# Moving two ScalarE-issued stores, of B and of the time step, later in the recorded program of a Mamba layer

## The chip, the cores and the metric

The kernel runs on one core of a Trainium2 chip. The metric is the device time of one execution in microseconds (us), and the kernel before and after the change are compared by medians of such times. All data are float32.

## The reference

Four layers are applied one after the other to an image `x` of shape (2, 128, 64, 64). The change lies in the last one, layer 3, a small selective-state-space model (Mamba) that runs over the channels of each pixel. The 128 channels of a pixel are a sequence of 8 tokens with 16 features. Cut to what matters:

```python
seq = x.transpose(0, 2, 3, 1).reshape(B * H * W, 8, 16)
xi, z = split(seq @ in_proj_w.T)                  # 32 inner features each
xs  = silu(causal_conv4(xi))
dt, Bm, Cm = split(xs @ x_proj_w.T, [1, 17])      # 1 + 16 + 16 columns
dt  = softplus(dt @ dt_proj_w.T + dt_proj_b)      # the time step
dA  = exp(dt[..., None] * A)                      # A = -exp(A_log), 16 states
dBx = dt[..., None] * Bm[:, :, None, :] * xs[..., None]
h_t = dA_t * h_{t-1} + dBx_t                      # 8 tokens, one after the other
y_t = sum over states of h_t * C_t
out = ((y + xs * D) * silu(z)) @ out_proj_w.T
result = x + silu(group_norm(out) * gn_gamma + gn_beta)
```

The layers before it are a Mamba over the image (layer 0) and two attention layers (1 and 2). The diff does not touch them.

## The kernel before

Layer 3 handles the 8192 pixels in 16 chunks of T = 512 pixels (`Chunk3`, called chunk 0 to chunk 15 here). A chunk holds two halves `i` of four tokens each, with 4 tokens x 32 inner features on the 128 partitions.

The scan over the 8 tokens is cut into 4 steps of two tokens (`PLACE`), so the main loop has 16 x 4 steps plus a few at the ends, counted by `s`. In a step the token pair needs the state-times-feature layout: 128 partitions hold 4 states x 32 features, and 4 groups of them cover the 16 states. Getting from one layout to the other means copying rows to many partitions, and this is done through device memory (DRAM):

- `b_` computes B on TensorE (into the PSUM tile `misc`) and copies it to `bs` on ScalarE, and ScalarE's queue stores it as the DRAM tile `rows` (256 KB, line L1193).
- `dt_add` adds the time step on GpSimd (L1217), and `put` stores it from ScalarE's queue as the DRAM tile `ddt` (512 KB, L1224).
- `spread(k)` (L1232) loads the time step of a token pair from `ddt` into `dtr`, in 8 DMAs of 64 KB (4 in step 0). `load(k, o)` (L1244) loads B of one token from `rows` into `D`, in 4 DMAs of 256 KB. Both are issued by SyncE (SP in the profile), two steps ahead of the step that uses them (`n2`).
- `da_` (L1273) makes the four exponentials `A` from `dtr` on ScalarE, one step ahead. `db_` (L1266) multiplies `D` with the time step times input on VectorE, also one step ahead.
- `mul` (L1283, GpSimd) and `add` (L1288, VectorE and GpSimd) carry the state over the tokens, and `hc_` (L1306, VectorE) and `y_` (L1316, TensorE) multiply by C and sum.
- In the first eight steps a 512 KB store of the input for later use, `kept` (L1483), is also issued by SyncE.

The order of the work is written by hand. The loop puts work in lists keyed by (step in chunk, quarter of the step): `first` runs at the start of a quarter, `extra` at its end, and `PLAN` orders the vector work in between. B and the time step of the next chunk (`fut`) are made in step 0 of the current one: `b_` in quarter 0, `put` in quarter 2. The lines are

```python
more((0, 0), fut.b_, at=first)
more((0, 1), fut.c_, at=first)
more((0, 2), fut.put, fut.cb_)
...
more((k, 0), lambda: n2.spread(n2k), lambda: n2.load(n2k, 0))
more((k, 1), lambda: n2.load(n2k, 1))
```

Two more things of the built program matter. First, each engine runs its own instructions in order. Second, the layer below the kernel's text (Tile) gives the DMAs of both issuing queues completion semaphores from one ring of eight, in the order in which it places the DMAs in the program. Before a DMA takes a semaphore, its issuing engine waits until the DMA that had the semaphore before, eight places earlier, has landed (a wait that the engine has already made is left out). So a DMA on SyncE can wait for a store that ScalarE issues, though it touches none of the same data.

Of the kernel before, what the change touches and what calls it, by code (L numbers as in the profile page):

```python
# [57 lines left out]
def conv_seq_kernel(ctx: ExitStack, tc: tile.TileContext, a: dict, out: bass.AP):  # L58
# [40 lines left out]
    with ExitStack() as c0:  # L99
# [9 lines left out]
        def wt(tag, bufs=None, shape=(P, 2, T)):  # L109
            return wk_.tile(list(shape), F32, tag=tag, name=tag, bufs=bufs)  # L110
# [386 lines left out]
        with tc.manual_schedule():  # L497
            c, c1 = chunks[:2]
# [234 lines left out]
    with ExitStack() as c1:  # L733
# [272 lines left out]
        for n, j in enumerate(jobs):  # L1006
# [10 lines left out]
            if jobs[n - 1].layer == 1:  # L1017
                for ci in range(NCH):
                    c = Conv(jobs[n - 1].b, ci)
# [70 lines left out]
    with ExitStack() as c3:  # L1090
# [61 lines left out]
        class Chunk3:  # L1152
# [35 lines left out]
            def b_(self):  # L1188
                p = self.bc_(0)
                self.bs = wt("bs", (P, T), bufs=1)  # L1190
                nc.scalar.copy(self.bs, p)
                self.rows = dr.tile([P, T], F32, tag="rows", name="rows")
                nc.scalar.dma_start(self.rows, self.bs)  # L1193

            def c_(self):
# [222 lines left out]
        with tc.manual_schedule():  # L1418
            mm(y, lhsT=ident, rhs=x[:, 0, 0:T], start=True, stop=True)
            c, c1 = chunks[:2]  # L1420
            for i in range(2):
                c.xs_(i)
            c.b_()
            for i in range(2):
                c.dt_(i)
            c.e_exp()
# [15 lines left out]
            for s in range(-1, len(steps) + 3):  # L1442
# [3 lines left out]
                fut = chunks[ci + 1] if s >= 0 and ci + 1 < len(chunks) else None  # L1446
# [8 lines left out]
                def more(key, *what, at=extra):  # L1455
                    at.setdefault(key, []).extend(what)

                if fut is not None:
                    more((0, 0), fut.b_, at=first)
                    more((0, 1), fut.c_, at=first)  # L1460
                    more((0, 2), fut.put, fut.cb_)
                if old is not None:
                    more((1, 0), lambda: old.yg_(1))
                    more((2, 1), old.xr_, at=first)
# [199 lines left out]
```

## Time and profile before

| what | value |
|---|---|
| median of 3 runs | 6684.76 us (6681.85 to 6688.01) |
| the profiled execution | 6684.23 us, of which the span on the core is 6682.4 us |
| busy over the span | PE 88%, DVE 83%, ACT 67%, POOL 81% |
| layer 3's loop, from the first `rows` store | from 5645 us to the end of the span |
| busy from 5640 to 6630 us (990 us) | PE 811.8, DVE 820.9, POOL 772.9, ACT 461.7 us |
| DMA in that stretch | 72% mean busy share of the 16 engines, 172 GB/s |
| `rows` stores, `ddt` stores | 16 and 16, all on ScalarE's queue |

The engine names are PE for TensorE, DVE for VectorE, ACT for ScalarE, POOL for GpSimd and SP for SyncE. A "q" behind a name is the engine's own instruction queue, where DMAs are issued and semaphores awaited. L1193 is line 1193 of the kernel before. Times within the run are microseconds from the start of the span. In the waits view, a row gives the waiting engine, the line, what it waited for, the total of that waiting, how often, and the longest. In the timeline, a row gives start, duration, engine, line, operation, tiles and, in brackets, idle time before it with what ended it. [...]

### The profile page before, as it was taken

What the parts mean: (1) busy time and instruction counts of PE and PEld (TensorE: products, weight loads), DVE (VectorE), ACT (ScalarE), POOL (GpSimd) and SP (SyncE); (2) the same over time, 40 slices, a digit from 0 to 9 for tenths busy, and PEclk for the clock granted to TensorE, in tenths of its full rate; (3) what the DMA queues carried; (4) which work ended last, traced back from release to release, by engine and by line L of the source; (5) the groups of instructions that cost most, each with busy time, mean ns of one, the idle gap of its engine ahead of it and who ended that gap; (6) DMA issues with size and microseconds to landing.
All of it is one profiled execution on the core that took longest, in us unless ns stands there. A gap on an engine that the chain in (4) does not pass through costs nothing. (4 is left out here: it accounts for less than half of the span.)

```text
span 6682.4 us, 66184 instructions
## 1 busy us (share of the span) xinstructions
PE 5857.7 (88%) x19918; PEld 2766.3 (41%) x19918; DVE 5536.6 (83%) x4462; ACT 4477.6 (67%) x7740; POOL 5404.5 (81%) x2473
## 2 busy tenths in 40 slices
PE   8888888888888888888879999999999997888787
PEld 2222222222222222222228887787788885222221
DVE  7999999999999999999986665565566765788888
ACT  7887788877788777887766664455455554444443
POOL 6999999999999999999986665555556665788787
PEclk7888778877788778887779999999999998788888
DMA  6666666566656666665640000000000001766765
GB/s 182 145 155 157 156 149 150 147 150 152 151 143 146 154 154 148 154 149 146 146 106 5 4 4 1 1 1 1 1 1 1 1 1 26 198 160 163 187 162 138
DMA packets 400473, 700.59 MB, mean 105 GB/s; under 512 B 74089, under 2 KB 76530, under 8 KB 399730
## 3 DMA queue, kind: packets, MB, share of 16 engines
q1 hardware_dynamic: 394624, 681.74, 42.1%
q10 hardware_dynamic: 5490, 14.63, 0.6%
q8 instruction: 156, 2.56, 0.2%
q14 instruction: 203, 1.66, 0.1%
HBM read 584.80 MB, written 111.28 MB: 104 GB/s over the span
## 5 line engine op out<-in xcount | busy, mean ns | idle before, releaser
L384 POOL TENSOR_TENSOR dbu<-dus,bs 128x1024 f32<-128x1024 f32 x1024 | 2459.6, 2437 | 101.0 <-DVE h L428 86.5
L428 DVE TENSOR_TENSOR_SCAN h<-da,hst,dbu 128x1024 f32<-128x1024 f32 x896 | 2091.4, 2341 | 94.1 <-ACT dbu L412 88.8
L397 ACT ACTIVATE da<-dts,aneg 128x512 f32<-128x512 f32 (+1 forms) x2048 | 1410.2, 689 | 350.2 <-DVE h L428 312.1
L924 POOL TENSOR_TENSOR sum<-sum,sc 128x1024 f32<-128x1024 f32 x384 | 906.0, 2360 | 492.1 <-ACT sc L919 488.3
L886 ACT COPY sc<-s 128x512 f32<-128x512 f32 x1024 | 597.0, 584 | 859.7 <-PE s L881 745.8
L893 DVE TENSOR_TENSOR mx<-mx,s 128x512 f32<-128x512 f32 x896 | 609.4, 680 | 546.3 <-ACT sc L886 545.0
L881 PE MATMUL s<-q,k 128*128 128x256 f32 x4096 | 1051.8, 380 | 6.4 <-ACT q L838 3.0
L451 PE MATMUL y<-hc,cst 128*32 128x512 f32 x4096 | 881.8, 757 | 198.6 <-DVE hc L440 179.3
L936 PE MATMUL av<-sc,v 128*128 128x256 f32 x4096 | 1048.6, 379 | 2.5 <-ACT sc L919 2.5
L440 DVE TENSOR_TENSOR hc<-h,pc 128x1024 f32<-128x1024 f32 x704 | 842.1, 1196 | 10.7 <-PE y L451 8.6
L881 PEld LDWEIGHTS s<-q,k 128*128 128x128 f32 x4096 | 776.7, 190 | 140.5 <-issue 29.0
L936 PEld LDWEIGHTS av<-sc,v 128*128 128x128 f32 x4096 | 768.2, 190 | 102.9 <-ACT sc L919 3.9
L438 POOL TENSOR_TENSOR hc<-h,cs 128x1024 f32<-128x1024 f32 x320 | 761.2, 2379 | 1.1 <-issue 1.1
L417 PE MATMUL pc<-xd,sel 16*128 16x512 f32 x1024 | 707.9, 782 | 1.5 <-DVE hc L440 1.3
L1283 POOL TENSOR_TENSOR A<-A,D 128x1024 f32<-128x1024 f32 x224 | 526.8, 2370 | 194.1 <-DVE D L1288 146.4
L916 DVE TENSOR_TENSOR sc<-sc,pm 128x1024 f32<-128x1024 f32 x512 | 620.3, 1212 | 0.9 <-PE pm L912 0.9
L919 ACT ACTIVATE sc<-sc 128x1024 f32<-128x1024 f32 x512 | 542.0, 1059 | 8.6 <-DVE sc L916 8.1
L341 PE MATMUL misc<-xd,w_dt 9*128 9x512 f32 x504 | 371.6, 825 | 141.9 <-ACT x L480 78.3
L451 PEld LDWEIGHTS y<-hc,cst 128*32 128x32 f32 x4096 | 125.4, 120 | 855.7 <-DVE hc L440 419.2
L412 ACT ACTIVATE dbu<-hst,dbu,df 128x1 f32<-128x1 f32 x896 | 337.9, 377 | 81.6 <-POOL dbu L384 59.0
L1266 DVE TENSOR_TENSOR D<-D,rx 128x1024 f32<-128x1024 f32 x224 | 268.6, 1211 | 143.9 <-DMA D<-rows 120.3
L1300 PE MATMUL q<-xs,lc 32*128 32x512 f32 x896 | 301.0, 678 | 64.9 <-DVE A L1306 63.9
(263 smaller groups left out, 7561.9 us busy)
## 6 DMA issues: line engine op xcount, KB each, us to landing
dts<-ddt SPq DMA_DIRECT2D x512, 256.0 KB, 5.5
dus<-ddu SPq DMA_DIRECT2D x512, 256.0 KB, 5.0
D<-rows SPq DMA_DIRECT2D x448, 256.0 KB, 6.0
bs<-rows SPq DMA_DIRECT2D x1024, 64.0 KB, 4.9
cs<-rows SPq DMA_DIRECT2D x1024, 64.0 KB, 3.3
ddt<-dt SPq DMA_DIRECT2D x128, 256.0 KB, 2.0
ddu<-dtu SPq DMA_DIRECT2D x128, 256.0 KB, 4.0
dtr<-ddt SPq DMA_DIRECT2D x448, 64.0 KB, 3.0
```

What stands on the lines that cost most here:

```text
L384: nc.gpsimd.tensor_mul(t, self.dus[q], _bc(self.bs[g], 1, [P, 2, T]))
L397: act(t[:, i, sl], self.dts[q][:, i, sl], AF.Exp, scale=an[:, g, 2 * q + i : 2 * q + i + 1])
L417: mm(t, lhsT=sel[32:48, 4 * g : 4 * g + 4, :].rearrange("p n d -> p (n d)"), rhs=self.xd[32:48, :], start=True, stop=True)
L428: nc.vector.tensor_tensor_scan(ho, ai, bi, init, ALU.mult, ALU.add)
L438: nc.gpsimd.tensor_mul(t, self.h[u], _bc(self.cs[gq(u)[0]], 1, [P, 2, T]))
L440: nc.vector.tensor_mul(t, self.h[u], _bc(self.pc[u // 2], 1, [P, 2, T]))
L451: mm(self.y[q // 2][r : r + 32, :], lhsT=sum4, rhs=self.hc[u][:, i, :], start=False, stop=(u % 8 >= 6), skip_group_check=True)
L881: mm(p[:, o, :], lhsT=j.k[m // 8][:, m % 8 * P : m % 8 * P + P], rhs=self.q, start=True, stop=True)
L893: nc.vector.tensor_max(self.mx, self.s[0][:, 0:2, :] if u == 1 else self.mx, self.p[u])
L916: nc.vector.tensor_sub(s, s, _bc(self.pm[:, :], 1, [P, 4, NQ]))
L924: nc.gpsimd.tensor_add(self.sum, self.s[0] if w == 1 else self.sum, self.s[w])
L936: mm(self.av, lhsT=self.job.v[m // 8][:, m % 8, :], rhs=self.s[u // 2][:, m % 4, :], start=(m == 0), stop=(m == 31))
```

## The change

The store of B is taken out of `b_` into a method of its own, `put_b`, and recorded in quarter 2 of step 0 instead of at the start of quarter 0. The store of the time step, `put`, is recorded in quarter 3 instead of quarter 2. The preamble for chunk 0 keeps its order.

```diff
                 self.rows = dr.tile([P, T], F32, tag="rows", name="rows")
+
+            def put_b(self):
                 nc.scalar.dma_start(self.rows, self.bs)
...
             c.b_()
+            c.put_b()
...
                     more((0, 0), fut.b_, at=first)
                     more((0, 1), fut.c_, at=first)
-                    more((0, 2), fut.put, fut.cb_)
+                    more((0, 2), fut.put_b, fut.cb_)
+                    more((0, 3), fut.put)
```

In the built programs the instructions of PE, DVE and POOL keep their order. On ACT, the store of B leaves its place between the copy to `bs` and the table load ahead of `da_`, and goes behind the four activations of `da_`, directly ahead of the store of the time step, which itself keeps its place on ACT. In the ring of semaphores the store of B moves back by one place in most chunks (by two in chunks 2 and 3, which have a `kept` store beside them, and by three in chunk 11), and the store of the time step keeps its place in every chunk.

## The prediction

> **What bounds the kernel now.** I read the waits of SP and DVE over layer 3's loop (5640 to 6630 us) first, to see who waits for the two stores.
>
> ```profile
> SPq L1232 <- DMA rows<-bs: 213.0, 13, 20.7
> ...
> SPq L1244 <- DMA rows<-bs: 31.8, 2, 16.1
> ```
> ```profile
> DVE D L1266 <- DMA D<-rows: 120.3, 22, 16.8
> ```
>
> SP waits for the store of B in 15 chunks, some 16 us each. DVE, the busiest engine of the loop, loses 120 us to late loads of `D`. The timelines of ACT and SP in one ordinary chunk (the stores of chunk 6) join the two.
>
> ```profile
> 5991.51 0.58 ACT L1191 COPY bs<-misc 128x512 f32<-128x512 f32 x1 [5.00 <-PE misc L1184]
> 5992.12 0.33 ACTq L1193 DMA_DIRECT2D rows<-bs  x1
> 5992.79 1.28 ACT L1273 ACT_TABLE_LOAD   x1 [0.69 <-ACT bs L1191]
> 5994.08 1.15 ACT L1273 ACTIVATE A<-dtr,aneg 128x1024 f32<-128x1024 f32 x1
> 5994.09 0.33 ACTq L1224 DMA_DIRECT2D ddt<-dt  x1
> ```
> ```profile
> 5970.30 5.39 SPq L1244 DMA_DIRECT2D D<-rows  x8
> 5994.20 5.48 SPq L1232 DMA_DIRECT2D dtr<-ddt  x8
> 5999.80 3.91 SPq L1244 DMA_DIRECT2D D<-rows  x8
> ```
>
> SP has issued everything ready by 5975.7 and then stands until 5994.2, when `rows` has landed. But that is not the wait that ends last. The chain of waits passes through the store of the time step:
>
> ```profile
> 5992.79 1.28 ACT L1273
> 5994.09 2.95 DMA ddt<-dt
> 5997.06 0.30 SPq L1232
> ...
> 6001.32 6.25 DMA D<-rows
> ...
> 6007.80 1.22 DVE D L1266
> ```
>
> Counting eight places in the ring of semaphores explains it. In an ordinary chunk the first `dtr` load of the next step (n0) waits for `rows`, n1 for a landed load, and n2 for `ddt`. Six `dtr` and four `D` issues follow the landing of `ddt`, then 6.25 us of transfer, and DVE, which ran dry 6.09 us earlier, goes on. Such a stall of 4.3 to 7.7 us stands once in each of chunks 1 to 15, so a microsecond on the landing of `ddt` is a microsecond on each chunk's period.
>
> **The change part by part.** The profiled execution took 6684.23 us (span 6682.4, 1.8 around it), 0.5 under the median of 6684.76; the sum below is made against 6684.23.
>
> *SP.* The stores move one place in the ring at most, and `ddt` none. After the change n0 waits for a landed load and n1 for `rows`; n2 still waits for `ddt`. SP gets n0 out some 16 us earlier and stands all the same. In an ordinary chunk the 16 us of waiting for `rows` vanish from that row and reappear as waiting for n1 and n2. Worth: 0. What covers it is the wait for `ddt`; without that cover the 3 us between the landings would count.
>
> *ACT, what goes.* The store of B no longer stands between the copy and the table load. Copy end to table load is 0.69 us, made of the 0.33 us issue and four semaphore waits on the queue. Those waits are for loads landed long before, so they now pass while the copy waits 5 us for PE. I take 0.02 us for the gap, as between other neighbours, so the activations of `da_` start 0.67 us earlier, at 5993.41. Their reader, POOL's `mul`, ended its wait on DVE, not on ACT, so this alone brings 0.
>
> *ACT, what comes.* `rows` is now issued behind the activations, right ahead of `ddt`. When does the queue get there? The row that tells is chunk 1, where the time step was ready on POOL at 5677.57 + 2.36 = 5679.93:
>
> ```profile
> 5687.19 1.15 ACT L1273 ACTIVATE A<-dtr,aneg 128x1024 f32<-128x1024 f32 x1
> 5687.20 0.33 ACTq L1224 DMA_DIRECT2D ddt<-dt  x1
> ```
>
> The store still left only when the first activation began. [...] The trace disagrees in nine chunks, so I follow the row: `rows` leaves at the start of the first activation (5993.41) and `ddt` one issue, 0.33 + 0.04 us, behind it at 5993.78. That is 0.31 us earlier than 5994.09.
>
> *The two transfers together.* So far `rows` had landed before `ddt` started. Now they run together. The median landings bound the price:
>
> ```profile
> ddt<-dt ACTq DMA_DIRECT2D x16, 512.0 KB, 3.0
> rows<-bs ACTq DMA_DIRECT2D x16, 256.0 KB, 2.0
> ```
>
> A further 256 KB cost about 0.95 us, so the data part of `rows` is about 0.95 us. If the engines work the two off in order, `ddt` loses 0.95 - 0.37 = 0.58 us. [...] No row of this trace shows two such stores at once. The lower end is 0 (full overlap), the upper a full serial landing (2.0 us ahead of 2.95). I take 0.58, nearest to the rows of one transfer. Net in an ordinary chunk: -0.31 + 0.58 = +0.27 us. Eight chunks (1, 5, 6, 7, 10, 12, 13, 15) are of this kind: +2.2 us.
>
> *Five chunks (4, 8, 9, 11, 14)* issued `ddt` 0.06 to 0.35 us after the first activation, when POOL's `dt_add` ended. `ddt` can't leave earlier there, and `rows`, 0.67 us earlier than that activation, has moved most of its 0.95 us of data by then: 0. In chunk 11 the store of B moves three places, among stores of the result, but the loads behind it wait for `ddt` (landed 6314.18) before and after.
>
> *Chunks 2 and 3.* There the `kept` store shifts the ring, and the last quarter of a `D` load waits for `rows` (the L1244 row above). SP held it until 5746.55, and the 512 KB of `kept` and that quarter then ran beside `ddt`. Counting 7 issues of 0.46 us back from the `D` issues at 5754.76 and 5817.34, `ddt` landed about 5751.4 and 5814.0: 4.6 and 3.9 us after its issue. After the change the quarter and `kept` leave some 16 us earlier, and `ddt` lands in about 3 us (chunk 2) and 3.5 us from an issue 0.33 earlier (chunk 3): -1.6 and -0.7 us. The 2.2 and 1.5 us that DVE lost to that quarter only lengthen the next stall, since `ddt` still decides. Together -2.3 us.
>
> *Queues moved past.* PE, DVE and POOL keep their order; no other DMA changes its queue. The first consumer of `rows` reads it some 20 us later (6012.7 against 5992.1), so its landing 1.3 us later is covered. `bs` is not written again for a chunk.
>
> Sum: +2.2 + 0 - 2.3 = 0 us. With full overlap in place of 0.58 it is -0.31 x 8 - 2.3 = -4.8. I say 6682.0, between, leaning on 0.
>
> *What the sum can't hold.* The chunk's period is not fixed. From copy to copy the windows of chunks 6 and 7 read
>
> ```profile
> 5992.10:6053.46 61.36, 50.61 (x160) 13.31 (x158) 53.62 (x43) 28.64 (x32) 49.47 (x21) 0.89 0.70 163
> 6053.46:6112.96 59.50, 52.78 (x160) 13.40 (x158) 52.09 (x43) 28.64 (x32) 48.17 (x21) 0.83 0.72 168
> ```
>
> with the same instructions. DVE's adds (L1288) are shorter in one (2.11 us mean against 2.32), by how they meet POOL's. A shift of 0.3 us on ACT and the loads may move chunks from one pattern to the other. That is ±1 us a chunk, ±10 us over the loop, and it carries most of the width.
>
> **The rivals.**
>
> *Faster: ACT's queue runs ahead.* If the store need not wait for the first activation, `ddt` leaves when both `rows` has been issued and POOL is done: about 1.0 us earlier in six of the eight chunks, 1.5 in chunks 1 and 10, 1.1 in chunk 3. With chunk 2's -1.6 that is -11.7 us: 6672. Chunk 1's row speaks against it. Chunks falling into the shorter period have the same sign: seven of them x 1.9 = -13. Chance that one or both pass 0.2%: 0.24.
>
> *Slower: the stores serialise.* If `ddt` lands a whole 2.95 us after `rows` has landed, ordinary chunks lose 2.01 + 2.95 - 0.67 - 2.95 = 1.34 us (eight: +11), the five others 1.0 (+5), chunks 2 and 3 about nothing: +16, 6700. It decides from about 1 us a chunk on, since 0.2% is 13.4 us. SP's loads, which overlap four deep, speak against it. With chunks falling into the longer period: 0.20.
>
> *Nothing happens.* The name says that the stores stand behind the loads, but `ddt`, the one that counts, keeps its place in the ring. This is my forecast: 0.56.
>
> **How the numbers follow.** About 0.2% (13.4 us) is what a measurement of this kernel can tell from no change. Same 0.56, faster 0.24, slower 0.20, from the three cases. The range takes both rivals' times as ends, with the period pattern's ±10 us and a little room: 6666 to 6702.
>
> **What would show it.** Right: `rows` and `ddt` issued 0.4 us apart at the first activation, the table load 0.02 us behind the copy, SP's wait for `rows` smaller by at most the part that `ddt`'s grows, one DVE stall of 5 to 8 us in each chunk, the L1244 wait for `rows` gone. Wrong: `ddt` landing more than 1 us earlier or later after the copy than 5.0 us (5992.1 to 5997.06), or DVE's wait for `D` away from 120 us by more than 13.

## The result and the profile after

The changed kernel takes 6690.27 us (median of 12 runs, 6679.49 to 6698.12), beside 6685.01 us (12 runs, 6678.43 to 6704.39) of the kernel before: a ratio of 1.0002, with a 95% interval of 0.9993 to 1.0012. No difference can be measured. A second set of 20 runs, beside another 39 of the kernel before, gave 0.9993 (0.9985 to 1.0001), so a gain of some 5 us can't be told from nothing by the times.

The profiled execution took 6696.6 us (span 6694.8), 12.4 us longer than the one of before. The traces say where these went, and it was not the place of the change. The waits of SP and of DVE, from 5640 to 6640 us (waiting engine, line, what it waited for: total, times, longest):

```profile
SPq L1234 <- DMA ddt<-dt: 1706.7, 15, 1691.7
SPq L1234 <- DMA rows<-bs: 227.6, 15, 21.4
```
```profile
DVE D L1268 <- DMA D<-rows: 109.3, 18, 16.4
```

The longest `ddt` wait, 1691.7 us, is SP standing ready through the layers before, and is taken off in every row of this kind: 15.0 us are left, 27.4 before. L1234 and L1246 are the lines of `spread` and `load` in the changed kernel, two further down than before. The row "L1244 waits for `rows`" has no successor. DVE's wait for `D` is 11 us shorter. Chunk 6 in the timelines of ACT and SP:

```profile
5988.37 0.58 ACT L1191 COPY bs<-misc 128x512 f32<-128x512 f32 x1 [5.01 <-PE misc L1184]
5988.98 1.28 ACT L1275 ACT_TABLE_LOAD   x1
5990.27 1.15 ACT L1275 ACTIVATE A<-dtr,aneg 128x1024 f32<-128x1024 f32 x1
5990.28 0.33 ACTq L1195 DMA_DIRECT2D rows<-bs  x1
5990.64 0.45 ACTq L1226 DMA_DIRECT2D ddt<-dt  x1
```
```profile
5967.12 5.28 SPq L1246 DMA_DIRECT2D D<-rows  x8
5974.87 21.36 SPq L1234 DMA_DIRECT2D dtr<-ddt  x8
5996.35 3.85 SPq L1246 DMA_DIRECT2D D<-rows  x8
```

The table load stands 0.03 us behind the copy. Both stores leave at the first activation, 0.36 us apart. SP spreads eight `dtr` issues over 21.36 us: it gets some out early, then stands, and its `D` issues begin 7.40 us after the end of the copy (5988.95), where they began 7.71 us after it before. DVE's stall behind them is still there:

```profile
6003.83 1.22 DVE L1268 TENSOR_TENSOR D<-D,rx 128x1024 f32<-128x1024 f32 x1 [5.28 <-DMA D<-rows]
```

The landings, as the DMA issues have them from 5640 to 6640 us (the last number is the median from issue to landing):

```profile
ddt<-dt ACTq DMA_DIRECT2D x16, 512.0 KB, 2.7
rows<-bs ACTq DMA_DIRECT2D x16, 256.0 KB, 2.0
```

To part the loop from what follows it, I read the copy to `bs` (L1191), which ACT makes once a chunk. From its start in chunk 1 to its start in chunk 15 is 14 periods; the rest, to the end of the span, is the last chunk and the normalisation. All kernels that were traced:

| kernel | 14 periods of the loop, us | the rest, us |
|---|---|---|
| before | 5684.69 to 6548.69: 864.0 | 133.7 |
| changed | 5684.26 to 6542.63: 858.4 | 152.2 |
| changed, profiled again | 5683.57 to 6540.80: 857.2 | 133.8 |
| both stores in step 1, quarter 0 | 5673.99 to 6483.71: 809.7 | 143.0 |
| both stores in step 1, quarter 1 | 5684.51 to 6510.77: 826.3 | 130.1 |
| the store of B three times as large | 5688.25 to 6565.18: 876.9 | 135.1 |
| only the time step later | 5685.89 to 6529.86: 844.0 | 147.3 |
| only B later | 5683.50 to 6541.62: 858.1 | 142.2 |
| no stores in the loop | 5686.06 to 6488.76: 802.7 | 142.9 |

The change made the loop 5.6 us shorter (6.8 in the second profile). The rest was 18.5 us longer in the first profile and as long as before in the second, with the same kernel. What differs there is TensorE. Three lines of its timeline after the last chunk's loads, changed and then before:

```profile
6643.88 1.92 PE L1302 MATMUL q<-xs,lc 32*128 32x512 f32 x4 [2.45 <-DVE A L1308]
...
6649.58 2.08 PE L1302 MATMUL q<-xs,lc 32*128 32x512 f32 x4
...
6672.90 5.34 PE L1318 MATMUL y<-A,cst 128*32 128x512 f32 x12
```
```profile
6644.74 2.08 PE L1300 MATMUL q<-xs,lc 32*128 32x512 f32 x4 [2.53 <-DVE A L1306]
...
6650.62 1.16 PE L1300 MATMUL q<-xs,lc 32*128 32x512 f32 x4
...
6663.10 2.77 PE L1316 MATMUL y<-A,cst 128*32 128x512 f32 x12
```

After an idle time of 2.5 us in both, the four matmuls to `q` take 1.92 to 2.08 us, at a granted clock of 0.50 (the share of its full clock that TensorE was allowed). Before, they were back at 1.13 to 1.16 us from 6650.6 on. In the changed kernel they stayed at 2.08 us, and the clock came back at about 6678, with TensorE busy throughout. One 10 us window of each shows it (the window and its length, then busy time and count of PE, PEld, DVE, ACT and POOL, then the granted clock, the DMA share and GB/s), changed and then before:

```profile
6660.00:6670.00 10.00, 10.00 (x22) 1.89 (x18) 2.71 (x3) 0.00 (x0) 0.00 (x0) 0.50 0.00 0
```
```profile
6660.00:6670.00 10.00, 8.10 (x32) 2.24 (x30) 4.55 (x6) 1.87 (x2) 0.00 (x0) 1.00 0.00 0
```

From the second `q` group shown to the end of the last line, the same matmuls take 28.7 us in the changed kernel (6649.58 to 6678.24) and 15.3 before (6650.62 to 6665.87). That is 13.4 of the 18.5 us. The other 5 were already lost at the first line shown, which stands 101.25 us after the last copy to `bs`, and 96.05 before. There was a second such stretch on the way: from 6582.6 to 6602.6 us the granted clock of this profile is 0.50, and at the same distance from the last copy it is 0.83 both before and in the changed kernel's second profile. That this cost the 5 us is likely, but not shown.

The other profiles fit. I read the granted clock near the end in windows of 10 us, for all but "both stores in step 1, quarter 1". Three windows in a row at 0.50 to 0.59 stand in four of these eight (the changed kernel's first, both stores in quarter 0, only the time step later, no stores). They have the four longest rests in the table, 142.9 to 152.2 us; the other four have 133.7 to 142.2.

### The profile page after: what moved, and what is told of

The parts are those of the page before. It is cut to its first block, busy times and chain, and to the rows that moved or that the text cites. A ratio compares the mean times of both kernels' runs of the same rounds, so it can differ in the third digit from the quotient of the medians.

```text
span 6694.8 us, 66185 instructions
## 1 busy us (share of the span) xinstructions
PE 5875.3 (88%) x19918; PEld 2768.8 (41%) x19918; DVE 5536.3 (83%) x4462; ACT 4477.5 (67%) x7740; POOL 5402.9 (81%) x2473
## 5 line engine op out<-in xcount | busy, mean ns | idle before, releaser
L1268 DVE TENSOR_TENSOR D<-D,rx 128x1024 f32<-128x1024 f32 x224 | 268.8, 1212 | 142.1 <-DMA D<-rows 109.3
```

## The experiments

Diffs are against the changed kernel. The theory to be tested is that of the prediction: SP's wait for the landing of `ddt`, through the ring of semaphores, sets the period, and the change leaves `ddt` where it was. The ring itself stands in the traces, which have the semaphore of each DMA: from 5640 to 6640 us the 922 DMAs of SP and the 32 stores of ACT share the same eight, before and after the change. SP's DMAs take them in turn, always in the same order, with 30 places left out in each kernel, and those are held by the 30 stores of chunks 1 to 15. In chunk 6 of the kernel before, `rows` has the semaphore that n0 takes next and `ddt` that of n2; in the changed kernel `rows` has that of n1, and `ddt` still that of n2. One rival is that the engines' own work sets the period and SP's waits are only a symptom of it. Another is that there was a gain, and that the two stores, now side by side on the DMA engines, hampered each other and ate it.

**The changed kernel once more**, beside the others, for the end of the run.

> The changed kernel once more, for a second profile. If the 12 us by which its profiled execution is longer than that of before come from where the lower granted TensorE clock falls in the last 90 us (0.50 to 0.59 from 6650 to 6680 us there, 0.96 to 1.00 in the profile of before), then the stretch from the first copy to bs of the loop to the last is again near 898 us, and the rest up to the end varies with the clock, between about 134 and 152 us. If the change itself lengthens the end, the end is again near 152 us at any clock.

It took 6686.14 us (20 runs), 0.9993 of the kernel before (0.9985 to 1.0001). Its profile has the loop at 857.2 us and the rest at 133.8. So the long end of the first profile is a matter of the execution, not of the change. (The clock of 0.96 to 1.00 in the profile of before holds to 6670 us; from 6670 to 6680 it was 0.56, with TensorE busy for 0.42 us.)

**Both stores in step 1, quarter 0.** This is what the name of the change says, done far enough: both stores stand behind the `dtr` and `D` loads that are recorded in step 0.

```diff
-                    more((0, 2), fut.put_b, fut.cb_)
-                    more((0, 3), fut.put)
+                    more((0, 2), fut.cb_)
+                    more((1, 0), fut.put_b, fut.put)
```

> Both stores are recorded at the end of quarter 0 of step 1 instead of step 0. In the ring of semaphores they now stand one whole step later: the loads of dtr and D for step 2 no longer wait for them, those for step 3 do. Theory A (the ring place of the time step's store decides, because its landing releases SP): the one stall of DVE per chunk before step 2, 5 to 8 us in each of 15 chunks, goes, and no equal one comes before step 3, because the store lands about 8.5 us after the copy to bs and D for step 3 is needed about 25 us after it. 70 to 95 us faster, about 6600. Theory B (the loads are late for want of DMA bandwidth or of free D buffers, whatever SP waits for): within 15 us of before.

It took 6620.5 us, 0.9897 of the kernel before (0.9881 to 0.9913): 1.0% or 68 us faster, just short of the 70 expected at least. The waits of SP and DVE in it:

```profile
SPq L1234 <- DMA ddt<-dt: 1695.0, 4, 1691.7
SPq L1234 <- DMA rows<-bs: 101.8, 13, 15.4
```
```profile
DVE D L1268 <- DMA D<-rows: 26.8, 3, 16.5
```

SP still waits for `rows`, 8 us in a chunk, but DVE hardly notices: within the 14 periods its wait for `D` is 10.3 us, where it was 86.0. The timeline of SP tells why:

```profile
5950.35 5.36 SPq L1246 DMA_DIRECT2D D<-rows  x8
5964.21 3.56 SPq L1234 DMA_DIRECT2D dtr<-ddt  x8
5967.86 1.79 SPq L1246 DMA_DIRECT2D D<-rows  x4
5969.75 1.76 SPq L1234 DMA_DIRECT2D dtr<-ddt  x4
```

The pause stands ahead of a group that goes on as `D` x4, `dtr` x4: only step 0 of a chunk has a `dtr` group of four, and only step 3 a `D` group of four, so the loads that wait are those of step 3 and of the next chunk's step 0. In the changed kernel the pause lies in a group that goes on as `D` x8, the loads of step 2. The wait was not removed but put one step further from its reader, and a step is about 15 us.

Of the 75.7 us that DVE no longer waits for `D`, the loop gives back only 48.7 (858.4 to 809.7). The groups of DVE over the 14 periods show the largest part of the rest, changed and then this kernel (count, then busy us, mean ns, idle before):

```profile
L1290 DVE TENSOR_TENSOR D<-D,A 128x1024 f32<-128x1024 f32 x112 | 244.0, 2179 | 0.1
```
```profile
L1290 DVE TENSOR_TENSOR D<-D,A 128x1024 f32<-128x1024 f32 x112 | 262.1, 2340 | 3.9 <-POOL A L1285 3.3
```

The same 112 adds took 18.1 us longer. The trace shows with what this goes. POOL works beside DVE, and an add that meets no POOL instruction takes 1.22 us, one that meets some takes up to 3.4. Two adds in this kernel's timeline (the first ends before POOL starts again at 5976.01):

```profile
5974.72 1.22 DVE L1290 TENSOR_TENSOR D<-D,A 128x1024 f32<-128x1024 f32 x1
...
5976.01 2.35 POOL L1285 TENSOR_TENSOR A<-A,D 128x1024 f32<-128x1024 f32 x1 [1.30 <-DVE D L1290]
...
5976.98 2.46 DVE L1290 TENSOR_TENSOR D<-D,A 128x1024 f32<-128x1024 f32 x1
```

Of the 112 adds 30 meet (almost) no POOL instruction in the changed kernel, and 19 here; the time in which an add and a POOL instruction run together grew from 159.7 to 179.4 us. Some 9 us went into other waits. The clock doesn't make the difference: granted over the 14 periods are 0.84 in the changed kernel and 0.87 here, and DVE's waits for TensorE's `q` are 23.7 and 22.4 us.

The medians lie 68 us apart, the loop 54 (864.0 to 809.7). Most of the 14 us between is the choice of executions: the two that were profiled lie 55.5 us apart (6684.23 and 6628.75), one 4.2 below and the other 8.3 above its median.

**Both stores in step 1, quarter 1**, one quarter further: does later go on being better?

```diff
-                    more((0, 2), fut.put_b, fut.cb_)
-                    more((0, 3), fut.put)
+                    more((0, 2), fut.cb_)
+                    more((1, 1), fut.put_b, fut.put)
```

> Both stores are recorded at the end of quarter 1 of step 1. In the ring they stand behind the D loads of step 2 and directly ahead of dtr for step 3; on ACT they are behind the activations for step 2, as in the run with quarter 0. Theory A: as that run, 70 to 95 us faster, and within 10 us of it, since D for step 3 waits for the store in both and is not needed soon. Theory B: within 15 us of before.

It took 6645.72 us, 0.994 of the kernel before (0.9918 to 0.9961): faster, but 25 us slower than the last run, where at most 10 us of difference was expected. The stores now leave ACT's queue 17.3 us after the copy, beside an activation of `xs_` that waited for TensorE (the timeline of ACT around chunk 6; the copy ended at 5973.23):

```profile
5972.65 0.58 ACT L1191 COPY bs<-misc 128x512 f32<-128x512 f32 x1 [2.25 <-PE misc L1184]
...
5990.48 0.69 ACT L1172 ACTIVATE xs<-misc,vec 128x512 f32<-128x512 f32 x1 [6.19 <-PE misc L1165]
5990.53 0.33 ACTq L1195 DMA_DIRECT2D rows<-bs  x1
5990.96 0.39 ACTq L1226 DMA_DIRECT2D ddt<-dt  x1
```

DVE waits 83.9 us for `D` in 18 stalls: with the stores so late, the loads behind them are late for the step after. The expectation had left out that the store stands behind this activation. Placing the stores one quarter further back moved their waiting loads back, but on ACT's queue they stood behind the activations recorded ahead of them: in chunk 6 `rows` left 17.3 us after the copy, where it left 1.8 us after it in the run with quarter 0, and its landing moved back as well.

**The store of B three times as large.** `rows` becomes a 768 KB store, right ahead of `ddt`; its later loads read one of the three copies.

```diff
-                self.rows = dr.tile([P, T], F32, tag="rows", name="rows")
+                wide = dr.tile([P, 3, T], F32, tag="rows", name="rows")
+                self.rows, self.wide = wide[:, 0, :], wide
...
-                nc.scalar.dma_start(self.rows, self.bs)
+                nc.scalar.dma_start(self.wide, _bc(self.bs, 1, [P, 3, T]))
```

> The changed kernel with the store of B three times as large (768 KB, the same row data written three times side by side; the loads read the first copy). It is issued directly ahead of the time step's store. Theory A: the time step lands later by the data time of 512 KB more, 1.3 us (at the rate that both stores together showed after the change) to 1.9 us (0.95 us per 256 KB), and each of 15 chunks loses that: 20 to 28 us slower than the changed kernel. Theory B, or stores that overlap freely: less than 8 us slower.

It took 6702.52 us (20 runs), 1.0018 of the kernel before (1.001 to 1.0027), and 16.4 us more than the changed kernel run beside it, some 4 us less than the 20 to 28 expected, and twice the 8 that the other case allowed. The source views of the two stores give their landings, `rows` and then `ddt`:

```profile
DMA to landing us min/median/max: 3.7/3.8/4.3
```
```profile
DMA to landing us min/median/max: 2.6/4.5/4.8
```

`ddt` lands 1.6 to 1.8 us later than in the changed kernel (2.7 and 2.9 in its two profiles), and the loop is 18.5 to 19.7 us longer than in those two profiles, 1.3 to 1.4 us each. So the later landing of `ddt` did lengthen the period, by about 0.8 us for each microsecond, which speaks against engines that set the period by themselves. The larger store ahead of `ddt` did delay it, which the rival of the hampered stores needs. What the one of 256 KB costs is worked out in the next section: 0.3 us a chunk at most, some 5 us over the loop. That can't have hidden a gain like the 54.3 us of the loop with both stores a step later.

**Only the time step later**, B as in the changed kernel:

```diff
-                    more((0, 3), fut.put)
+                    more((1, 0), fut.put)
```

> The changed kernel with the store of the time step alone moved on, to the end of quarter 0 of step 1; the store of B stays where the change put it, and n2 of the dtr loads for step 2 now waits for it. Theory A (SP is released by whichever store still stands eight places ahead of those loads): SP is released when B has landed, about 1.3 us earlier than when the time step had, so each of 15 chunks gains about 1.3 us: 15 to 25 us faster than before, not 68. If only the time step's landing counts, this run gains the whole 68 us of the run with both moved.

It took 6677.09 us, 0.9969 of the kernel before (0.9958 to 0.998): 12.4 us faster, below the 15 to 25 expected.

```profile
SPq L1234 <- DMA rows<-bs: 213.0, 15, 20.7
```

SP goes on at the landing of `rows`, and the loop is 14.4 us shorter than the changed kernel's, 1.0 a period. About as much lies between the two landings there: 1.06 us by the medians (5990.28 + 2.0 and 5990.64 + 2.7), 1.3 in chunk 6 itself, where `ddt` took 2.9.

**Only B later**, the time step where it was before the change:

```diff
-                    more((0, 2), fut.put_b, fut.cb_)
-                    more((0, 3), fut.put)
+                    more((0, 2), fut.put, fut.cb_)
+                    more((1, 0), fut.put_b)
```

> The changed kernel with the store of B alone moved on, to the end of quarter 0 of step 1; the store of the time step is recorded in quarter 2 of step 0, as before. Theory A: SP waits for the time step as before; without B ahead of it on ACT's queue it leaves 0.3 to 0.4 us earlier than in the changed kernel in some chunks. 0 to 12 us faster than before.

It took 6673.29 us, 0.9976 of the kernel before (0.9964 to 0.9988): 16.2 us faster, where 0 to 12 were expected.

```profile
SPq L1234 <- DMA ddt<-dt: 1923.6, 15, 1691.8
SPq L1234 <- DMA rows<-bs: 39.4, 14, 4.0
```

The wait for `rows` has gone over to `ddt` (231.8 us without the long one), and the loop is the changed kernel's to 0.3 us (858.1). So in this profile moving the store of B alone does not move the loop. It isn't free, though: `rows` now runs among SP's loads and takes 6.4 us to land in place of 2.0 (medians), SP has a new wait of 39.4 us for it, and `ddt`, which leaves up to 0.37 us earlier in the chunks where it had followed `rows`, brings nothing.

The times say something else than the loop. Why the median is 12.9 us below that of the changed kernel run in the other set, I can't say: the profiled execution was the slowest of the seven (6685.56 us), with an end of 142.2 us, and the others were not traced. By the medians the store of B alone (16.2 us) gained no less than the time step alone (12.4), with intervals that overlap. That the time step counts and B does not rests on one profile of each.

**No stores in the loop.**

```diff
-                self.rows = dr.tile([P, T], F32, tag="rows", name="rows")
+                self.rows = dr.tile([P, T], F32, tag="rows", name="rows") if self is chunks[0] else chunks[0].rows
...
             def put_b(self):
+                if self is not chunks[0]:
+                    return
...
             def put(self):
+                if self is not chunks[0]:
+                    self.ddt = chunks[0].ddt
+                    return
```

> B and the time step of chunks 1 to 15 are not stored; all chunks load those of chunk 0 (this leaves out 15 stores of each kind and with them the right data of those chunks). It is the upper bound of what the stores cost, by waits and by traffic. Theory A: as the run with both stores a step later, or a little more: 65 to 85 us faster. If the traffic of the stores or ACT's issue of them costs something of its own, more than that.

It took 6616.83 us, 0.9886 of the kernel before (0.987 to 0.9903), with 802.7 us for the 14 periods: 72.7 us faster, as expected. What the two stores cost by waits and traffic together is 61.3 us of loop. Moving both by one step brought 54.3 of it. What is left is close to DVE's own work: in the 14 periods without stores DVE is busy 761.0 us, 95%, PE 88% and POOL 86%.

## Why the prediction was right

*The time.* 6682.0 was forecast as "same"; the median came out 8 us above it and, with the second set of runs, within 0.1% of the kernel before both times. That forecast covered anything within some 13 us of the kernel before, so it did not need the small terms of the sum to be right. Whether they were, only the traces tell.

*`ddt` decides, and keeps its place.* Shown by the loops of the profiles. Moving the time step alone took 1.0 us off each period, and the wait passed to `rows`, which landed about as much earlier; moving both removed the stall; moving B alone left the loop where it was, though the times of that run don't bear this out. That "a microsecond on the landing of `ddt` is a microsecond on each chunk's period" was a little too round: 1.6 to 1.8 us on the landing gave 1.3 to 1.4.

*ACT.* In chunk 6 it came as worked out: the table load 0.66 us earlier relative to the copy (0.03 for 0.69 us behind its end), the stores at the first activation (1.33 us after the copy's end), 0.36 us apart, and `ddt` 0.31 us earlier than before. The row of chunk 1 was the right one to follow, over the faster rival's "the store need not wait for the first activation": before, no `ddt` of chunks 1 to 15 left ahead of the first activation (nine left 0.01 us after its start, the others 0.06 to 0.36), and in the changed kernel `rows` left 0.01 us after it in 14 chunks and 0.06 in chunk 11. Why a store waits there, the runs do not show. But the sum gave these 0.31 us to eight chunks, and in the first profile only four of them (1, 6, 10, 12) got them, or nearly. In chunk 7 of the changed kernel the time step itself was late:

```profile
6049.50 0.33 ACTq L1195 DMA_DIRECT2D rows<-bs  x1
6050.51 0.33 ACTq L1226 DMA_DIRECT2D ddt<-dt  x1
```
```profile
6048.11 2.37 POOL L1219 TENSOR_TENSOR dt<-dt,e 128x1024 f32<-128x1024 f32 x1
```

`ddt` left when POOL had made it (6048.11 + 2.37), 2.32 us after the copy's end (6048.19), where it had been 2.00 before. So it was in chunks 13 and 15, while chunks 8 and 14, counted at 0, gained 0.6 to 0.7. Which chunks are "ordinary" depends on how the copy falls beside POOL's work, and the change moved that too.

*The overlap of the two stores: mis-sized.* The step "I take 0.58, nearest to the rows of one transfer" failed. That two stores are worked off in order, on which the 0.58 was built, was an assumption, which no run shows. In chunk 6 `rows` still lands in 2.0 us and `ddt` in 2.9, where the chain of before has 2.95, so the step's price against the kernel before is 0, its lower end. But that row of before was not of a store alone. There the landing of `rows` released two loads of SP at 5994.2, which ran beside `ddt`; now it releases one, and `rows` is the other neighbour:

```profile
5992.31 0.31 SPq L1234 DMA_DIRECT2D dtr<-ddt  x1
```

The landing of `ddt` in chunk 6 of the changed kernel, and in chunk 6 of the run with only B later, where it has no such neighbour:

```profile
DMA to landing us min/median/max: 2.9/2.9/2.9
```
```profile
DMA to landing us min/median/max: 2.6/2.6/2.6
```

So `rows`, 0.36 us ahead, and one load cost `ddt` some 0.3 us together, where 0.58 was forecast for `rows` by itself. In chunk 7, with `rows` 1.01 us ahead, it is 2.7; the median of 2.7 mixes the two kinds. With 768 KB ahead the cost was 1.6 to 1.8 us.

*The sum.* With full overlap it is the -4.8 us that stood as its other end; measured were -5.6 and -6.8. That they are so close is in part luck, since the eight chunks were not the right eight. What does hold is the link: in the 14 chunks whose landing the traces have, `ddt` landed on average 5.24 us after the copy before and 4.88 after it in both profiles of the changed kernel, which is 5 us over 14 periods. Chunk 2 has the largest part: its landing of 4.7 us became 2.7, a gain of 2.0 where 1.6 was forecast.

*SP's rows.* Wrong in two details. The 16 us of a chunk were to "vanish from that row" of waits for `rows`; but n1 waits for `rows` as n0 did, and the row went from 213.0 to 227.6. With the second line of before (244.8 together) it shrank, though not "by at most the part that `ddt`'s grows": that for `ddt` shrank as well, from 27.4 to 15.0. The price of 0 put on it held, since `ddt` still landed after `rows`.

*The signs.* The L1246 wait for `rows` is gone, and a stall of 4.1 to 7.7 us (5 to 8 were named) stands in each of chunks 1 to 15 of the first profile. One sign of being wrong came true: DVE's wait for `D`, to be within 13 us of 120, was 109.3 in the first profile but 100.1 in the second. It fits a change that gained a little, as the loop shows, more than one that gained nothing.

*What the sum couldn't hold.* The ±10 us were laid to the period's two patterns, by how DVE's adds meet POOL's. That adds are longer where they meet POOL is so (1.22 us without it). But the loop of one and the same kernel differed by only 1.2 us in two profiles. The width of this kernel's times is elsewhere, in large part at the end: 18.4 us between those same two.

## What to carry to other kernels

Where DMAs of several queues take their completion semaphores from one set, as the two queues do here (eight in the traces), find the DMA whose landing ends the wait, and ask which load takes its semaphore next and how long that load can be late. Moving a store is worth something when it moves the wait to loads with more time to spare, and little when only a neighbour that lands earlier is moved. And part a trace at a mark that recurs (here one copy a chunk) before a difference of two executions is read as the work of a change.

## What the runs showed of the hardware

- TensorE's granted clock fell to 0.50 near the end in both kernels after an idle time of 2.5 us. In one execution (before) it was at 1.00 again some 6 us after the matmuls went on, in another (changed) only some 34 us after; what decides between the two, the runs do not show. In the stretch measured this cost 13.4 us, more than twice what the change did to the whole loop.
- Two stores from one queue, 256 KB and then 512 KB: the second landed in 2.9 us when issued 0.36 us behind the first (with one 64 KB load beside them), in 2.7 when 1.01 us behind, and in 2.6 without the first. With 768 KB ahead it took 4.5 us. Among SP's loads the same stores took longer: 6.4 us in place of 2.0 for the 256 KB (only B later), 7.5 for the 512 KB (only the time step later; medians).
- The adds of DVE took 1.22 us where they met no POOL instruction and up to 3.4 where they did. As DVE waited less they met POOL more and became slower (2.18 to 2.34 us mean), which took back 18 of 76 us. By what the two engines hamper each other, the runs do not show.
- In the trace of before, SP, ACT, DVE and POOL went through their instructions in the order of the built program, compared line by line: 4504 DMAs on SP, 7740 instructions and 39 DMAs on ACT, 4454 instructions on DVE, 2468 on POOL. For TensorE the trace does not show it.
